# Telling a kernel's own list scheduler how VectorE and GpSimd share an SBUF port, with durations and due times set anew

## The chip, the cores and the metric

One core of one Trainium2 chip. The metric is the device time of one execution in microseconds (us), lower is better. "Before" and "after" are the two kernels; L1023 is line 1023 of the kernel at hand, and lines move by five between before and after.

## The reference, cut to what matters

Four graph layers over 128 graphs of 64 nodes with 256 features, in float32:

```python
h = relu(layernorm(x)); x = x + attention(h, adj)             # layer 0: 8 heads, masked by adj
h = relu(layernorm(x)); x = x + attention(h, log(adj + 1e-6)) # layer 1
h = relu(layernorm(x)); x = x + ggnn(h, adj)                  # layer 2: 5 steps of aggregate and GRU
h = relu(layernorm(x)); x = x + elu(gated_gcn(h, adj))        # layer 3
```

The graphs are handled in 16 groups of four pairs. Three groups are in work at any time: one in its attention layers ("front"), one or two in their GRU steps, one in layer 3 ("back"). Names in the lines below: q, k, v, s, e and aT belong to attention (aT is a transpose of the weights e on TensorE), agg to the aggregation over neighbours, gb, gc, nb, nc and sn to the GRU, l3b, l3c and F to layer 3, lnT, hT and hx are transposes, xn is a normalised input. SBUF and PSUM are the two on-chip memories; in this kernel TensorE's results land in PSUM.

## The kernel before

The kernel records every operation with an engine, an estimated cost, its inputs and outputs and a due time ("key"), and a list scheduler in the kernel then decides in which order the operations are emitted. In the runs below each engine takes its operations in the order in which they were emitted: in swap1, where 11 VectorE operations were each moved by one place, only these and the ones they passed change place in the trace. So all of the argument is about numbers that the scheduler believes:

```python
AFTER = {"PE": 210, "DVE": 125, "ACT": 145, "POOL": 90, "SP": 2500}   # ns until a result is seen
TO_PE = 120
BESIDE = 0.2      # weight for a tiled matmul block next to another
TURNING = 0.05
AHEAD = 1.75      # how far past the most urgent key an operation may be placed, in groups
FRONT_SPAN = 0.9  # ... due times of fronts, backs, GRU steps, first groups, fused weights ...
BACK_LAST = 0.85
STEP_SPAN = 0.4
BACK_END = -0.05
FIRST = -1.0

def dve(n, ptr=0):
    return n * 1.042 + 75 + 60 * ptr

# class Plan, run(): one step of the list scheduler
for eng, ops in ready.items():
    for op in ops:
        if op.key > horizon:
            continue
        at = max(clock[eng], op.ready)
        if op.port:                     # GpSimd, and VectorE with two SBUF inputs or in a 2-port mode
            at = max(at, locked["POOL" if eng == "DVE" else "DVE"])
        # ... buffers ...; among those that can start within 15 ns of the first, the most urgent
op.fn()                                 # emits the instruction
end = at + op.cost
if op.port:
    locked[op.eng] = end + 60
```

Operations from the attention layers, the GRU update and layer 3:

```python
vec(120, ... nc.vector.reciprocal(z.tile, z.tile))                    # L766, 128x8
pool(1000, ... nc.gpsimd.tensor_tensor(e8(), e8(), z..., op=ALU.mult))  # L767, then PE transposes e: "aT"
vec2(dve(TOK), ... scalar_tensor_tensor(a_(), a_(), 0.5, b_(), ...))  # L1023; vec2 = needs the port
sca(... Tanh ...)
pool(1230, ... nc.gpsimd.tensor_tensor(b_(), hh(), a_(), op=ALU.subtract))   # L1027
vec2(dve(TOK, 1), ...)                                                # L1029
vec2(dve(TOK, 0.5), ...)                                              # L1031
vec(dve(384), ... tensor_tensor(F..., part(bk), t..., op=ALU.add))    # L1195: one input in PSUM, no port
```

## Time and profile before

| | before |
|---|---|
| time, median of 4 runs | 2582.32 us (2581.43 to 2583.26) |
| span of the profiled run | 2579.5 us |
| TensorE busy | 2526.5 us |
| one group in the repeating part | 156.64 us |

How to read it: PE is TensorE (PEld its weight loads), DVE is VectorE, ACT ScalarE, POOL GpSimd. A group of lines gives the busy time, the mean duration in ns, and after the second bar the idle time of the engine before those instructions and what ended it. A line of the waits gives the waiting operation, what it waited for, the total, the number of times and the longest. TensorE's waits from 400 to 2200 us, the repeating part, are only these:

```profile
PE aT L773 <- POOL e L767: 6.8, 12, 0.6
PE l3c L1183 <- DVE F L1195: 6.1, 11, 0.6
PE qkvc L669 <- DVE v L690: 2.8, 12, 0.2
PE gc L918 <- DVE sg L990: 2.4, 12, 0.4
PE hT L509 <- DVE h L1031: 0.3, 1, 0.3
```

Four waits come back in every group, at the same places. They add up to 18 us of recorded idle.

### The profile page before, as it was taken

The page shows a single profiled execution, that of the slowest core. Times are in us where ns is not written, and L with a number is a line of the kernel's source. Part 1 is how long each engine was busy: PE and PEld are TensorE (multiplying, and loading weights), DVE is VectorE, ACT ScalarE, POOL GpSimd, SP SyncE. Part 2 cuts the span into 40 slices and gives each one's busy share as a digit, 9 for nine tenths or more (in the row PEclk, how much of TensorE's full clock was granted, in tenths as well). Part 3 has the DMA queues.
Part 4 walks back from the last instruction along what each step waited for, and adds up shares of the span by engine and source line. Part 5 has one row for each costly group of instructions (what it writes and reads, how often), then busy time and mean ns, then how long its engine had stood idle before and what let it go on. Part 6 is the DMA issues. An engine that isn't in the chain of part 4 may idle for free.

```text
span 2579.5 us, 58085 instructions
## 1 busy us (share of the span) xinstructions
PE 2526.5 (98%) x23489; PEld 2144.7 (83%) x23489; DVE 2086.3 (81%) x4647; ACT 1401.4 (54%) x2796; POOL 856.8 (33%) x890
## 2 busy tenths in 40 slices
PE   8999999999999999999999999999999999999997
PEld 6788888888888888888888888888888888888885
DVE  5876787888888888888878878888888888876766
ACT  3555555555555555555555565555555555555543
POOL 4533323324323243323323233243232333323220
PEclk9999999999999999999999999999999999999998
DMA  6331222113131122222212221121211122111110
GB/s 207 117 111 53 70 69 78 65 53 99 48 99 62 64 70 69 78 70 69 67 60 78 70 82 64 54 95 48 99 62 64 66 70 78 65 52 65 48 69 17
DMA packets 78256, 188.47 MB, mean 73 GB/s; under 512 B 14802, under 2 KB 66852, under 8 KB 67108
## 3 DMA queue, kind: packets, MB, share of 16 engines
q1 hardware_dynamic: 77872, 184.71, 21.3%
q8 instruction: 186, 3.05, 0.5%
q14 instruction: 82, 0.67, 0.1%
q10 hardware_dynamic: 116, 0.04, 0.0%
HBM read 166.70 MB, written 18.02 MB: 72 GB/s over the span
## 4 chain that ended last, share of the span: by engine, by line
PE 87%; DVE 9%; ACT 2%; issue 1%; POOL 1%; DMA 0%; ACTq 0%; POOLq 0%; DVEq 0%
PE gb L918 19%; PE gc L918 15%; PE nb L918 10%; PE nc L918 7%; PE qkvb L669 5%; PE y L805 4%; PE qkvc L669 4%; PE agg L958 3%; PE s L731 3%; PE l3b L1183 2%; PE hT L509 2%; PE l3c L1183 2%; PE lnT L509 2%; PE o L792 2%; PE aT L773 2%
## 5 line engine op out<-in xcount | busy, mean ns | idle before, releaser
L1027 POOL TENSOR_TENSOR sn<-h,sn 128x512 f32<-128x512 f32 x160 | 212.4, 1328 | 592.7 <-ACT sn L1025 580.9
L918 PE MATMUL gb<-Th,w_hh 128*128 128x256 f32 x960 | 250.6, 383 | 0.3 <-DVE sg L990 0.3
L918 PE MATMUL gb<-Ta,gv 128*128 128x256 f32 x960 | 246.9, 380 | 0.0
L767 POOL TENSOR_TENSOR e<-e,ssum 128x512 f32<-128x512 f32 x128 | 142.2, 1122 | 278.8 <-DVE ssum L766 240.8
L495 POOL TENSOR_TENSOR rstd<-pw,few 128x2 f32<-128x2 f32 x128 | 104.7, 819 | 357.3 <-DVE pw L494 351.4
L887 POOL TENSOR_TENSOR Th<-h 128x256 f32<-128x256 f32 x160 | 116.3, 747 | 311.9 <-PE nb L918 174.7
L918 PEld LDWEIGHTS gb<-Th,w_hh 128*128 128x128 f32 x960 | 174.3, 190 | 26.2 <-issue 0.8
L918 PEld LDWEIGHTS gb<-Ta,gv 128*128 128x128 f32 x960 | 176.1, 190 | 21.3
L918 PE MATMUL gc<-h,w_hh 128*128 128x256 f32 x640 | 167.4, 384 | 0.1
L918 PE MATMUL gc<-agg,gv 128*128 128x256 f32 x640 | 164.4, 379 | 0.0
L535 DVE TENSOR_SCALAR xn<-x,mv,rstd 128x256 f32<-128x256 f32 x256 | 125.4, 525 | 31.1 <-POOL rstd L495 15.6
L1029 DVE SCALAR_TENSOR_TENSOR sn<-sg,sn 128x512 f32<-128x512 f32 x160 | 109.5, 684 | 50.6 <-POOL sn L1027 50.5
L1010 ACT ACTIVATE sg<-sg,b_rz 128x512 f32<-128x512 f32 x160 | 109.3, 716 | 74.3 <-DVE sg L990 74.3
L1025 ACT ACTIVATE sn<-sn,b_n 128x512 f32<-128x512 f32 x160 | 115.4, 722 | 56.6 <-DVE sn L1023 55.9
L1021 DVE SCALAR_TENSOR_TENSOR sn<-sg,sn 128x512 f32<-128x512 f32 x160 | 135.8, 849 | 12.3 <-ACT sn L1075 7.8
L918 PE MATMUL nb<-Th,w_hh 128*128 128x256 f32 x480 | 144.6, 383 | 0.0
L918 PE MATMUL nb<-Ta,gv 128*128 128x256 f32 x480 | 143.1, 380 | 0.0
L887 POOL TENSOR_TENSOR Th<-h,Th 128x256 f32<-128x256 f32 x160 | 138.1, 863 | 11.5 <-DVE h L1031 5.8
L805 PE MATMUL y<-w_L_gnn_Wo,oT 128*128 128x256 f32 x512 | 135.1, 383 | 0.5 <-DVE oT L800 0.5
L918 PEld LDWEIGHTS gc<-agg,gv 128*128 128x128 f32 x640 | 119.3, 190 | 17.9 <-issue 0.2
L1031 DVE SCALAR_TENSOR_TENSOR h<-sn 128x512 f32<-128x512 f32 x160 | 128.4, 802 | 2.8
L1023 DVE SCALAR_TENSOR_TENSOR sn<-sn 128x512 f32<-128x512 f32 x160 | 128.4, 802 | 0.9
(207 smaller groups left out, 6832.7 us busy)
## 6 DMA issues: line engine op xcount, KB each, us to landing
gv<-gates SPq DMA_DIRECT2D x80, 1344.0 KB, 5.8
qw<-kept SPq DMA_DIRECT2D x203, 192.0 KB, 2.4
x<-in_x_dram SPq DMA_DIRECT2D x32, 256.0 KB, 3.0
out_dram<-x SPq DMA_DIRECT2D x32, 256.0 KB, 2.5
gates<-gv SPq DMA_DIRECT2D x5, 1344.0 KB, 5.2
adjq<-in_adj_dram SPq DMA_DIRECT2D x8, 256.0 KB, 3.0
gw<-in_L_gnn_weight_dram SPq DMA_DIRECT2D x5, 256.0 KB, 5.9
kept<-s SPq DMA_DIRECT2D x8, 128.0 KB, 1.8
```

What stands on the lines that cost most here:

```text
L535: vec2(325, lambda p=p, i=i: nc.vector.tensor_scalar(xn[:, i, :], xt[:, p, :], mv[:, i, 0:1], rstd[:, i : i + 1], op0=ALU.subtract, op1=AL ...
L669: nc.tensor.matmul(bk[:, j * P : (j + 1) * P], lhs, rhs, start=first and j == 0, stop=True, skip_group_check=True)
L767: pool(1000, lambda e8=e8, z=z: nc.gpsimd.tensor_tensor(e8(), e8(), z[:, :, None].to_broadcast(shape), op=ALU.mult), [e, z], [e])
L805: pe(mm(256), lambda i=i, c=c: nc.tensor.matmul(py[:, i * D : (i + 1) * D], oT[:, i, c, :], w_o[:, c, :], start=c == 0, stop=c == 1), [(oT ...
L887: pool(690, lambda: nc.gpsimd.tensor_tensor(T[:, i, :], x(), y(), op=ALU.subtract), reads, [(T, i)])
L918: nc.tensor.matmul(bank_[:, col * HALF : (col + 1) * HALF], at(g, n), rhs(), start=first and j == 0, stop=True, skip_group_check=True)
L1021: vec2(dve(TOK), lambda: nc.vector.scalar_tensor_tensor(a_(), r(), 1.0, a_(), op0=ALU.add, op1=ALU.mult), [*ts[0], n_v], [n_v])
L1023: vec2(dve(TOK), lambda: nc.vector.scalar_tensor_tensor(a_(), a_(), 0.5, b_(), op0=ALU.mult, op1=ALU.add), [n_v], [n_v])
L1025: sca(act(TOK, 1.5), lambda: nc.scalar.activation(a_(), a_(), AF.Tanh, bias=b_n[:, oc : oc + 1]), [n_v, b_n], [n_v])
L1027: pool(1230, lambda: nc.gpsimd.tensor_tensor(b_(), hh(), a_(), op=ALU.subtract), [*hp, n_v], [n_v])
L1029: vec2(dve(TOK, 1), lambda: nc.vector.scalar_tensor_tensor(b_(), z(), 1.0, b_(), op0=ALU.add, op1=ALU.mult), [*ts[1], n_v], [n_v])
L1031: vec2(dve(TOK, 0.5), lambda: nc.vector.scalar_tensor_tensor(hh(), b_(), 0.5, a_(), op0=ALU.mult, op1=ALU.add), [n_v], hp)
```

## The change

Its intent: a scheduler that expects port conflicts where they happen. GpSimd now counts as asking for the port when its data is there (it is picked first and delayed then), holds end a little before the operations do, the tiny power operations hold the port only at their start, costs are brought nearer to the recorded ones, and the weights, the run-ahead and all due times are set anew. No operation is added or removed.

```diff
-TO_PE = 120
+TO_PE, TO_POOL = 120, 60
+HOLD = {"DVE": 60, "POOL": 95}
-BESIDE = 0.2
+BESIDE = 0.5
-TURNING = 0.05
-AHEAD = 1.75
+TURNING = 0.15
+AHEAD = 2.15
-FRONT_SPAN = 0.9
+FRONT_SPAN = 0.95
-BACK_LAST = 0.85
-BACK_SPAN = 0.6
+BACK_LAST = 0.45
+BACK_SPAN = 0.65
-STEP_SPAN = 0.4
+STEP_SPAN = 0.5
-BACK_END = -0.05
-ENTRY = 0.05
-FIRST = -1.0
-FIRST_SPAN = 1.1
+BACK_END = 0.1
+ENTRY = 0.25
+FIRST = -1.2
+FIRST_SPAN = 1.15
-FUSE_SPAN = 0.45
+FUSE_SPAN = 0.4
-    return n * 1.042 + 75 + 60 * ptr          # dve
+    return n * 1.042 + 68 + 60 * ptr
-    return n * 0.833 + 70 + 90 * ptr          # act
+    return n * 0.833 + 60 + 105 * ptr
-        return op.lat
+        return op.lat + (TO_POOL if user.eng == "POOL" and op.eng == "DVE" else 0)
-                    if op.port:
-                        at = max(at, locked["POOL" if eng == "DVE" else "DVE"])
+                    if op.port and eng == "DVE":
+                        at = max(at, locked["POOL"])
             op.fn()
+            if op.port and op.eng == "POOL":
+                at = max(at, locked["DVE"])
-                locked[op.eng] = end + 60
+                locked[op.eng] = end - HOLD[op.eng] if op.port == 1 else at
-        pool(680 if n == 2 else 1220, ... op=ALU.pow
+        pool(660 if n == 2 else 970, ... op=ALU.pow ... port=2)
-        pool(1560, ... bias addition
+        pool(1225, ... bias addition
-                vec2(dve(TOK, 1), ...
+                vec2(dve(TOK), ...
 ... (further costs: bn_stats, bn_aggr, reciprocal, one activation, a copy, the vec2 of L1031)
```

More of the change, by code (lines that the diff above doesn't have):

```diff
@@ L309, in sca, with pool @@
         plan.add("ACT", cost, fn, reads, writes, early=early)
-    def pool(cost, fn, reads, writes, early=0.0):
-        plan.add("POOL", cost, fn, reads, writes, early=early, port=True)
+    def pool(cost, fn, reads, writes, early=0.0, port=1):
+        plan.add("POOL", cost, fn, reads, writes, early=early, port=port)
     def dma(kb, fn, reads, writes, n=1):
@@ L494, in power @@
         vec2(70, lambda: nc.vector.tensor_scalar(s.tile, at(), eps, None, op0=ALU.add), [src], [s])
-        pool(680 if n == 2 else 1220, lambda: nc.gpsimd.tensor_tensor(dst.tile, s.tile, few[:, 1 : 1 + n], op=ALU.pow),
-             [s, (few, 1)], [dst])
+        pool(660 if n == 2 else 970, lambda: nc.gpsimd.tensor_tensor(dst.tile, s.tile, few[:, 1 : 1 + n], op=ALU.pow),
+             [s, (few, 1)], [dst], port=2)
     def transposed(dst, dst_at, src, src_at, name, on_act, writes, relu=False, early=0.0,
@@ L528, in norm_relu_t @@
             p = 2 * half + i
-            vec(345, lambda p=p, i=i: nc.vector.bn_stats(st[:, i, :], xt[:, p, :]), [(xt, p)], [(st, i)])
-            vec(95, lambda i=i: nc.vector.bn_aggr(mv[:, i, :], st[:, i, :]), [(st, i)], [(mv, i)])
+            vec(332, lambda p=p, i=i: nc.vector.bn_stats(st[:, i, :], xt[:, p, :]), [(xt, p)], [(st, i)])
+            vec(83, lambda i=i: nc.vector.bn_aggr(mv[:, i, :], st[:, i, :]), [(st, i)], [(mv, i)])
         power(rstd, mv, lambda: mv[:, :, 1], EPS, 2, name)
@@ L743, in attend @@
             pe(860, scores, [qk, k_exp], pss, holds=es, mode=T64)
-        pool(1560, lambda: nc.gpsimd.tensor_tensor(
+        pool(1225, lambda: nc.gpsimd.tensor_tensor(
             xt[:, pp : pp + 2, :], xt[:, pp : pp + 2, :], bo[:, None, :].to_broadcast([P, 2, D]),
@@ L765, in attend @@
                 [e], [z])
-            vec(120, lambda z=z: nc.vector.reciprocal(z.tile, z.tile), [z], [z])
+            vec(109, lambda z=z: nc.vector.reciprocal(z.tile, z.tile), [z], [z])
             pool(1000, lambda e8=e8, z=z: nc.gpsimd.tensor_tensor(
@@ L1016, in update @@
                             last, lambda k=k: last[:, k * HALF : (k + 1) * HALF])
-                        sca(act(HALF, 1), lambda k=k, col=col, half=half, at=at: nc.scalar.activation(
+                        sca(act(HALF, 1.4), lambda k=k, col=col, half=half, at=at: nc.scalar.activation(
                             g_v[:, half, k, :], at(), AF.Tanh, bias=b_rz[:, col : col + 1], scale=0.5),
@@ L1028, in update @@
                      [*hp, n_v], [n_v])
-                vec2(dve(TOK, 1), lambda: nc.vector.scalar_tensor_tensor(
+                vec2(dve(TOK), lambda: nc.vector.scalar_tensor_tensor(
                     b_(), z(), 1.0, b_(), op0=ALU.add, op1=ALU.mult), [*ts[1], n_v], [n_v])
-                vec2(dve(TOK, 0.5), lambda: nc.vector.scalar_tensor_tensor(
+                vec2(dve(TOK), lambda: nc.vector.scalar_tensor_tensor(
                     hh(), b_(), 0.5, a_(), op0=ALU.mult, op1=ALU.add), [n_v], hp)
@@ L1108, in front @@
             s = slice(gp * NODES, (gp + 1) * NODES)
-            pool(530, lambda s=s: nc.gpsimd.tensor_copy(blk[s, :, s], adjq[s, sel, :]), [adjq], [(blk, gp)])
+            pool(350, lambda s=s: nc.gpsimd.tensor_copy(blk[s, :, s], adjq[s, sel, :]), [adjq], [(blk, gp)])
         A = new("A", [P, PAIRS, NODES], 3, f"A_{g}")
```

## The prediction

> **What bounds the kernel now.** I read the page's engine table, then the chain of work that ended last, then TensorE's waits and its timeline over one repeating stretch, then the groups of VectorE and GpSimd.
>
> ```profile
> PE 2526.5 (98%) x23489; PEld 2144.7 (83%) x23489; DVE 2086.3 (81%) x4647; ACT 1401.4 (54%) x2796; POOL 856.8 (33%) x890
> ...
> PE 87%; DVE 9%; ACT 2%; issue 1%; POOL 1%; DMA 0%; ACTq 0%; POOLq 0%; DVEq 0%
> ```
>
> TensorE (PE) is busy 98% of 2579.5 us and makes up 87% of the chain. A gain must therefore come out of TensorE's gaps, or from cheaper matmuls. Its busy figure hides part of the gaps, because a matmul's recorded span reaches over the start of the next one; so I price matmuls by the distance between starts. The timeline of TensorE in the repeating part (start, time, engine, line, operation, tile, count, idle before) shows both a price and a gap:
>
> ```profile
> 1245.09 1.03 PE L918 MATMUL gb<-Ta,gv 128*128 128x256 f32 x4
> 1245.95 0.59 PE L918 MATMUL nb<-Th,w_hh 128*128 128x256 f32 x2
> 1246.38 0.60 PE L773 MATMUL aT<-ident,e 128*128 128x128 f32 x4
> 1247.22 0.71 PE L669 MATMUL qkvc<-hTQ,qw 128*128 128x128 f32 x4 [0.24 <-DVE v L690]
> 1247.77 0.39 PE L669 MATMUL qkvc<-qw,hTQ 128*128 128x128 f32 x2
> 1248.72 0.66 PE L773 MATMUL aT<-ident,e 128*128 128x128 f32 x4 [0.56 <-POOL e L767]
> ```
>
> Four 256-column matmuls take 0.86 us from start to start, 0.216 each. The four transposes at 1246.38 should take 4 x 0.109 = 0.44 and the next work starts 0.84 later: a 0.40 us gap, of which the record calls 0.24 idle. Priced like this over the whole trace (medians: 0.216, 0.111, 0.322 and 0.429 us for 256, 128, 384 and 512 columns, 0.109 for a transpose; tiled blocks by their means, 0.015, 0.027 and 0.011 us for agg, s and o, plus about 0.1 to enter a tiled block and 0.14 to 0.19 to leave it), TensorE's work is: 1,632 us of 256-column matmuls, 266 of 128, 135 of 384, 24 of 512, 191 of transposes, 175 of tiled ones, 48 of mode changes: **2472 us**. Outside it lie 8.3 us before the first matmul, about 8 after the last, and some **92 us of gaps**. By part of the run, counting only gaps over 40 ns: 19 in the first 400 us, 46 from 400 to 2200, 3 to 2500, 18 in the tail.
>
> From 400 to 2200 us the chain repeats: 128x256 blocks of gc stand at 836.49, 993.10, 1149.78 and 1306.39 us, so one group of four graph pairs takes 156.6 us. Its priced work is 152.3, so **4.3 us per group are gaps**. TensorE's waits between 993.10 and 1149.78 us, which is one such group:
>
> ```profile
> PE aT L773 <- POOL e L767: 0.6, 1, 0.6
> PE l3c L1183 <- DVE F L1195: 0.6, 1, 0.6
> PE gc L918 <- DVE sg L990: 0.3, 2, 0.2
> PE qkvc L669 <- DVE v L690: 0.2, 1, 0.2
> ```
>
> By starts, these four are 0.73, 0.73, 0.33 and 0.40 us; an hT transpose adds 0.26, and eleven gaps of 0.10, each with a wait just before it, nearly all the rest.
>
> **What the Trainium skill says.** (1) SBUF — State Buffer, section Who interferes with whom: VectorE and GpSimd share one port pair; it is an exclusive lock, and a VectorE instruction with two SBUF inputs or in a 2-port mode and a GpSimd instruction that reads SBUF block each other in the order of issue. The trace agrees. Groups of 128x512 VectorE operations with equal shapes:
>
> ```profile
> L1029 DVE SCALAR_TENSOR_TENSOR sn<-sg,sn 128x512 f32<-128x512 f32 x160 | 109.5, 684 | 50.6 <-POOL sn L1027 50.5
> L1021 DVE SCALAR_TENSOR_TENSOR sn<-sg,sn 128x512 f32<-128x512 f32 x160 | 135.8, 849 | 12.3 <-ACT sn L1075 7.8
> L1031 DVE SCALAR_TENSOR_TENSOR h<-sn 128x512 f32<-128x512 f32 x160 | 128.4, 802 | 2.8
> ```
>
> L1029 waits for GpSimd's result, so it rarely meets a GpSimd operation: 684 ns. L1021 and L1031 meet them: means 849 and 802, with medians of 689 and 684 and maxima above 1600. The same happens to GpSimd: the multiplication at L767 has a median of 1043 ns, and took 1.51 us just before the 0.56 us wait above. That wait is port contention reaching TensorE. (2) Perfetto Trace Analysis, section Tensor Engine Instruction: TensorE's end times are estimated from the instruction's size, not observed. The trace agrees (four matmuls "1.03 us" long start 0.86 us apart), which is why starts are used. (3) The same page, section GPSIMD Engine Instruction, advises against trusting a GpSimd span. Here medians and minima differ by 1% (1272 and 1262 ns at L1027), so I use them, but with care.
>
> **The change, part by part.** No instruction is added or removed. Each engine has as many instructions in the built program as before (12,621 on TensorE, 4649 VectorE, 2804 ScalarE, 895 GpSimd); only their order moves, on every engine. The order is made by a list scheduler in the kernel, and the change makes its inputs truer.
>
> - Costs: the GpSimd subtraction stays 1230 ns (median 1272), the bias addition goes from 1560 to 1225 (1322 measured), the small powers from 680/1220 to 660/970 (706/1017), a block copy from 530 to 350 (398). VectorE's fixed part drops from 75 to 68.
> - Port: before, the scheduler held GpSimd back until VectorE had let the port go when choosing what to place, and added 60 ns to every hold. Now GpSimd asks when its data is there, the hold ends 60 or 95 ns before the operation does, and the tiny powers hold it only at their start (they take 706 ns for two columns). This should stop the scheduler's surprises, such as the 1.51 us multiplication.
> - Weights for staying in a tiled mode, due times, a longer run-ahead (1.75 to 2.15 groups).
>
> *Cost of TensorE's work.* I counted mode changes in both built orders. Entries into tiled blocks from plain work: 169 before, 175 after; switches between the two tile sizes 38 and 31. At the prices above, 48.3 against 48.6 us. So the stronger preference for tiled neighbours buys nothing: **+0.3 us**, and one group's work becomes 152.4 us.
>
> *The gaps of the repeating part.* The new order repeats exactly from group to group; the old one alternates slightly. What I can count is how much TensorE work lies between a producer and its consumer. For l3c's second product after the first, whose wait cost 0.73 us, it is 1.3 us before and 1.5 after, and to the third 0.9 before and 3.0 after. From agg to the first gb product on Ta the smallest distance is 5.1 before and 9.4 after; from the hT transpose to agg 1.8 and 3.1. In layer 0's second half the distance from s to aT falls from 9.3 to 7.3, but VectorE has less queued there (10 operations, 6.1 us of medians, instead of 14 and 7.5). Against that, qkvc still has a turnaround of 1.7 us in one half (as the one that cost 0.40), and one aT now stands 16.1 us behind s with 16.5 us of VectorE medians between (before, such sums came out some 15% above the measured time: 8.3 for 7.0 us). I judge that half of the 4.3 us goes: 2.1 us a group left. Over 13 groups that repeat or nearly do: 13 x 2.1 = **-27 us**.
>
> *Head and tail.* The first agg block comes after 103.3 us of priced work instead of 104.8: about -1. In the tail the last GRU product of the last group ends 19.6 us of work before the end instead of 21.1, and from it to the end runs a chain of 42 us that filler does not shorten: **+1.5**. One transpose that waited 1.31 us moves behind other work: **-1**. Sum: 2581.7 + 0.3 - 27 - 1 + 1.5 - 1, so about **2555**; I put 2557, as re-tuning to a model seldom gains all it promises.
>
> **Rivals.** (a) *The gaps only move.* VectorE is busy 85% of a group (132.5 of 156.7 us), its own waits are short, and a scheduler that packs it against 1.7 us turnarounds may create as many misses as it mends. For it: the old scheduler also believed its plan. Against it: the sizes put in are nearer the records. It would make 2575 to 2590. (b) *All gaps go.* For it: they are few, the same in each group, and each under 0.75 us. Against it: 37 us of head and tail come from data dependencies. At most 13 x 4 = 52 us, so 2530. (c) *A longer run-ahead starves something:* buffers or the queue of weight loads make TensorE wait for DMA. Against it: only 8.3 us of TensorE's waits are for DMA, all before the first matmul, and DMA is 21% busy. It would cost 10 to 30 us.
>
> **Range and chances.** The gap left per group decides: 0.8 us gives about 2538, 3.8 about 2577. So 2538 to 2577, eight times in ten. Faster by 2% needs under 2530, which is rival (b) in full and more: 0.03. Slower by 2% means 51 us more gaps: 0.01.
>
> **What would show it right or wrong.** Right: equal instruction counts, a group period of 154 to 155.5 us, TensorE's busy time nearly unchanged with gaps at aT and l3c gone, VectorE's L1021, L1023 and L1031 (moved by five lines) with lower means. Wrong: a period of 156 or more with waits under new names (rival a), waits for DMA (c), or a head or tail that changes by over 8 us.

## The result, and the profile after

The changed kernel takes **2537.85 us** (median of 4 runs, 2536.72 to 2538.85) against 2582.32: 44.5 us less. Ratios here are the mean time of one kernel's runs over that of the other's of the same rounds, so not quite the ratio of the medians: 0.9828, 95% interval 0.9811 to 0.9845. The predicted time was 2557, and the measured one lies just outside the low end of the range.

The head of the page of after:

```profile
PE 2507.0 (99%) x23489; PEld 2142.7 (85%) x23489; DVE 2047.8 (81%) x4647; ACT 1396.5 (55%) x2796; POOL 865.1 (34%) x890
...
PE 95%; DVE 3%; ACT 1%; DMA 0%; issue 0%; POOL 0%; SPq 0%; DVEq 0%; ACTq 0%; POOLq 0%
```

As many instructions, and the chain is now 95% TensorE instead of 87%. The busy times of the engines from 400 to 2200 us (PE, PEld, DVE, ACT, POOL, granted clock, DMA share, GB/s), first before, then after:

```profile
400.00:2200.00 1800.00, 1780.63 (x16914) 1522.94 (x16913) 1521.54 (x3348) 1004.17 (x2022) 601.90 (x609) 1.00 0.21 70
```

```profile
400.00:2200.00 1800.00, 1800.00 (x17224) 1552.16 (x17223) 1488.01 (x3415) 1016.36 (x2066) 613.97 (x617) 1.00 0.22 72
```

After, TensorE is busy for all of the 1800 us, does 310 more matmuls in them, and its list of waits there is empty. VectorE does 67 more operations in 33.5 us less.

By starts of the first agg block of each group, the 44.6 us between the two profiled spans divide like this (us):

| part of the run | before | after | difference |
|---|---|---|---|
| start to the third group | 360.6 | 355.5 | -5.1 |
| third to thirteenth group (ten groups) | 1565.0 | 1537.1 | -27.9 |
| thirteenth to sixteenth | 427.8 | 424.6 | -3.2 |
| sixteenth to the last matmul | 218.4 | 210.3 | -8.1 |
| last matmul to the end | 7.7 | 7.4 | -0.3 |

Waits are not all that changed in the head and the tail. The profile also records the granted clock, the share of its full clock that TensorE was given (third figure from the end in these lines). Two of the four stretches of before, ahead of its last matmul, in which it was about half; then, in after, the same stretch of the head, and the tail up to its last matmuls:

```profile
45.10:51.90 6.80, 5.93 (x76) 4.48 (x77) 2.12 (x4) 0.99 (x2) 6.57 (x7) 0.50 0.65 204
2547.00:2550.40 3.40, 3.40 (x7) 1.71 (x6) 1.61 (x3) 0.98 (x2) 0.00 (x0) 0.51 0.18 62
```

```profile
45.10:51.90 6.80, 6.45 (x54) 4.66 (x55) 4.96 (x13) 1.68 (x4) 6.80 (x7) 1.00 0.68 186
2500.50:2530.70 30.20, 21.62 (x78) 12.33 (x76) 27.20 (x82) 13.27 (x29) 2.91 (x3) 1.00 0.08 27
```

The other two stretches of before are 2512.9 to 2516.3 and 2557.3 to 2560.7 us. Matmuls in them take twice their price: the pair of 384 columns at 2548.17 us starts 1.28 us before the next pair, 0.64 for each, against 0.322. By these prices the half clock costs before about 3.2 us in the head, 1.7 between the sixteenth group and the last GRU product, and 3.1 behind that product; after, nothing. So by this estimate some 8 of the 44.6 us are clock and not waits. In all profiled runs such stretches stand only before 160 us or after 2480 us; those of before come behind waits of TensorE of 2.1, 1.4, 4.6 and 1.8 us, and its repeating part, whose longest wait is 0.6 us, has none. That the waits bring the clock down was not tested.

One group takes 153.93 us instead of 156.64, with 152.43 priced as before. The VectorE groups that the prediction pointed to, after:

```profile
L1026 DVE SCALAR_TENSOR_TENSOR sn<-sg,sn 128x512 f32<-128x512 f32 x160 | 119.9, 757 | 38.5 <-ACT sn L1080 35.7
L1028 DVE SCALAR_TENSOR_TENSOR sn<-sn 128x512 f32<-128x512 f32 x160 | 114.2, 720 | 1.5
L1036 DVE SCALAR_TENSOR_TENSOR h<-sn 128x512 f32<-128x512 f32 x160 | 109.7, 692 | 2.6
L976 DVE TENSOR_TENSOR Ta<-agg,Ta 128x256 f32<-128x256 f32 x160 | 97.8, 611 | 1.5
```

The three operations of the GRU update fall to 757, 720 and 692 ns (849, 802 and 802 before). But the subtractions that make Ta rise from 456 to 611 ns. Counting every VectorE operation that took over 100 ns more than the 15th percentile of its kind, 288 were lengthened before, by 189 us in all, and 308 after, by 139 us; on GpSimd 187 by 67 us and 250 by 73 (a kind is one line, one set of tiles, one shape). Every one of them overlaps an operation of the other engine. **There are not fewer port conflicts, though together they cost 44 us less of the two engines' time. From 400 to 2200 us TensorE waits for none of them.**

### The profile page after: what moved, and what is told of

It reads as the page before. It is cut to its first block, busy times and chain, and to the rows that moved or that the text cites.

```text
span 2534.9 us, 58088 instructions
## 1 busy us (share of the span) xinstructions
PE 2507.0 (99%) x23489; PEld 2142.7 (85%) x23489; DVE 2047.8 (81%) x4647; ACT 1396.5 (55%) x2796; POOL 865.1 (34%) x890
## 4 chain that ended last, share of the span: by engine, by line
PE 95%; DVE 3%; ACT 1%; DMA 0%; issue 0%; POOL 0%; SPq 0%; DVEq 0%; ACTq 0%; POOLq 0%
PE gb L923 22%; PE gc L923 16%; PE nb L923 11%; PE nc L923 8%; PE qkvb L674 6%; PE qkvc L674 5%; PE y L810 4%; PE agg L963 3%; PE l3b L1188 3%; PE s L736 3%; PE l3c L1188 2%; PE hT L514 2%; PE lnT L514 2%; PE aT L778 2%; PE o L797 2%; PE hom L1251 1%
## 5 line engine op out<-in xcount | busy, mean ns | idle before, releaser
L1032 POOL TENSOR_TENSOR sn<-h,sn 128x512 f32<-128x512 f32 x160 | 207.3, 1299 | 549.2 <-ACT sn L1030 549.2
L892 POOL TENSOR_TENSOR Th<-h 128x256 f32<-128x256 f32 x160 | 126.6, 811 | 243.8 <-PE nb L923 166.5
L1026 DVE SCALAR_TENSOR_TENSOR sn<-sg,sn 128x512 f32<-128x512 f32 x160 | 119.9, 757 | 38.5 <-ACT sn L1080 35.7
L1034 DVE SCALAR_TENSOR_TENSOR sn<-sg,sn 128x512 f32<-128x512 f32 x160 | 109.5, 690 | 40.0 <-POOL sn L1032 39.6
L976 DVE TENSOR_TENSOR Ta<-agg 128x256 f32<-128x256 f32 x160 | 90.0, 578 | 55.5 <-PE nb L923 43.5
L923 PEld LDWEIGHTS gc<-h,w_hh 128*128 128x128 f32 x640 | 117.8, 190 | 16.4 <-ACT sg L1022 0.5
L987 ACT ACTIVATE p5g<-gc 128x512 f32<-128x512 f32 x80 | 47.7, 596 | 145.7 <-PE gc L923 102.3
```

The lines of the kernel that those rows point to most:

```text
L892: pool(690, lambda: nc.gpsimd.tensor_tensor(T[:, i, :], x(), y(), op=ALU.subtract), reads, [(T, i)])
L923: nc.tensor.matmul(bank_[:, col * HALF : (col + 1) * HALF], at(g, n), rhs(), start=first and j == 0, stop=True, skip_group_check=True)
L1026: vec2(dve(TOK), lambda: nc.vector.scalar_tensor_tensor(a_(), r(), 1.0, a_(), op0=ALU.add, op1=ALU.mult), [*ts[0], n_v], [n_v])
L1032: pool(1230, lambda: nc.gpsimd.tensor_tensor(b_(), hh(), a_(), op=ALU.subtract), [*hp, n_v], [n_v])
L1034: vec2(dve(TOK), lambda: nc.vector.scalar_tensor_tensor(b_(), z(), 1.0, b_(), op0=ALU.add, op1=ALU.mult), [*ts[1], n_v], [n_v])
```

## The experiments

Two theories at the start. A: the truer model of the port and the durations removed the gaps, whatever the due times. B: the new due times and run-ahead made the gain, and the model is only along. A third, C: each order is a draw, and the result is the best of many. Gains below are given as ratios to the kernel before, run on the same chip in the same rounds (its medians: 2582.43, 2581.45, 2581.65 and 2581.54 us in the four sets); the changed kernel stands at 0.9828. Every output was correct.

### Which part of the change: the model or the due times

Only the model (port rule and costs), with the old weights, run-ahead and due times:

```diff
 # before, with
+TO_POOL, HOLD, the new port rule, port=2, all new costs
```

> New port rule and new durations, with the weights, due times and run-ahead of before. Theory A (a truer model of the port and the durations removes the gaps, whatever the due times): group period near 154 us in the mean of two groups (the order alternates), gaps of TensorE over 40 ns in the repeating part 1 to 2 us a group, time 2540 to 2550. Theory B (the newly set due times and run-ahead made the gain, the model is only along): period 156 to 157, time 2575 to 2585. Theory C (each order is a draw; the result is the best of many): anything, also slower than before.

Measured: 2587.04 us, ratio 1.0018 (1.0002 to 1.0035). No gain at all. By parts: a group takes 155.61 us in the mean (156.64 before), and the ten groups from the third to the thirteenth take 1551.2 us, 13.8 less; but the third group's agg comes at 383.5 us instead of 360.6. TensorE's longest wait in the first 360 us, apart from the first load, is this:

```profile
PE aT L778 <- POOL e L772: 11.6, 3, 6.5
```

Three transposes wait 11.6 us for GpSimd's multiplication in the first groups (2.9 before). That is 8.7 of the 22.9 us; other waits make some 6.5, and 6 are clock: 27.3 us of this head run at half clock, 6.8 before. Theory A falls as stated.

Only the weights, run-ahead and due times, with the old model:

```diff
 # before, with
+BESIDE, TURNING, AHEAD and all due times of after
```

> Weights, due times and run-ahead of after, with the old port rule and old durations. Theory A: period 156 to 157 us, four gaps of 0.3 to 0.7 us a group left at aT, l3c, gc or qkvc, time 2570 to 2582; only head and tail shorter. Theory B: period near 154, time 2538 to 2548. Theory C: anything.

Measured: 2566.49 us, ratio 0.9939 (0.9924 to 0.9954); a group takes 155.57 us. Neither theory: 16 us of the 44.5.

Without the port rule, and without the costs:

```diff
 # after, with
-HOLD, TO_POOL, the new port rule and port=2      (port_old)
 # after, with
-all new costs                                    (durations_old)
```

> The changed kernel with the old port rule and old holds alone put back. If the port rule is what counts: most of the gaps return, period 155.5 to 157, time 2562 to 2580. If the durations count instead: period about 154, time within 8 us of the changed kernel (2530 to 2546).

> The changed kernel with the old durations alone put back. If the durations are what counts: period 155.5 to 157, time 2562 to 2580. If the port rule counts: period about 154, time 2530 to 2546. If both are needed: both this and the run with the old port rule lie about half-way, 2550 to 2565.

Measured: port_old 2568.25 us, ratio 0.9946, 154.99 us a group; durations_old 2552.33 us, ratio 0.9885, 154.66 us a group. With the new due times, the costs alone bring nothing (2566.5 to 2568.3), the port rule alone 14 us (2566.5 to 2552.3), and the costs on top of the port rule another 14 us (2552.3 to 2537.9). So the parts act together. The trace qualifies this for the repeating part: there the costs alone do bring 0.6 us a group (155.57 to 154.99), lost again in the head and behind the thirteenth group.

The runs so far suggest a fourth theory, D: model and due times gain only together. Whether the due times of the repeating part belong to this:

```diff
 # after, with
-FRONT_SPAN = 0.95, BACK_SPAN = 0.65, STEP_SPAN = 0.5, ENTRY = 0.25
+FRONT_SPAN = 0.9, BACK_SPAN = 0.6, STEP_SPAN = 0.4, ENTRY = 0.05
```

> The changed kernel with the due times of the repeating part put back (front, back and step spans, entry). Theory A (model and due times act each by itself): period 154 to 154.5, time 2538 to 2548. Theory D (the truer model needs due times set to it, the two act together): period 155 to 156.6, time 2552 to 2580.

Measured: 2559.34 us, ratio 0.9914 (0.9899 to 0.9928), 155.61 us a group, the same as model_new_dues_old. Both figures lie where theory D (the two parts need each other) put them, but D holds only in part: in the repeating part the new model alone gives 1.0 us a group, the new due times alone 1.1, both 2.7, so most of that gain adds up and 0.6 us a group needs both. What needs both above all is the head, which the new model alone lengthens by 23 us.

### Head and tail

```diff
 # after, with
-FIRST = -1.2, FIRST_SPAN = 1.15, FUSE_SPAN = 0.4
+FIRST = -1.0, FIRST_SPAN = 1.1, FUSE_SPAN = 0.45      (head_old)
 # before, with the new model and
+FIRST = -1.2, FIRST_SPAN = 1.15, FUSE_SPAN = 0.4      (model_new_head_new)
```

> The changed kernel with the due times of the first groups and of the weight fusing put back (-1.0, 1.1, 0.45). Only rows 12 to 1290 of TensorE differ. If these made the 5 us of the head: third group's agg at 360 us or later instead of 355.5, time 2543 or more; since the new model with all old due times reached it at 383.5, up to +28 is possible (2565). If the head owes its gain to the model: within 2 us of 2538.

> New port rule and durations with the old weights, run-ahead and due times, but the new due times of the first groups and of the weight fusing. The same kernel without these lost 23 us before the third group. If that loss comes from due times that do not fit the truer model: agg of the third group at 355 to 362 us instead of 383.5, time 2558 to 2566. If it comes from the run-ahead or the weights: 380 us or later, time about 2585.

Measured: head_old 2551.84 us, ratio 0.9884; the third group's agg at 369.8 us instead of 355.5, and all later parts as in after within 0.1 us. model_new_head_new 2564.12 us, ratio 0.9933; 359.1 us instead of the 383.5 of the same kernel with the old head. So the 23 us that the new model lost there were due times that did not fit it, and three numbers gave them back. In head_old's 14.3 us, 8 are recorded waits and 5.8 are matmuls in 13.7 us at half clock.

```diff
 # after, with
-BACK_LAST = 0.45, BACK_END = 0.1
+BACK_LAST = 0.85, BACK_END = -0.05
```

> The changed kernel with the two due times of the last backs put back (0.85 and -0.05). In the built order only the last 68 of 12,621 rows of TensorE and the last 96 of VectorE differ. If these two due times shortened the tail: last GRU product to the end 41 us again instead of 34.4, time +6 to +8, so 2544 to 2546. If the tail got shorter by the truer costs or by what stands before it: within 2 us of 2538.

Measured: 2549.79 us, ratio 0.9877 (0.9862 to 0.9892). The time from the last GRU product to the end, 41.7 us before and 34.4 after, is 47.0 here, worse than in either, and 12 us instead of the 6 to 8 expected. TensorE's waits from 2440 us on, first in after, then in tail_old:

```profile
PE l3b L1188 <- ACT hT L519: 2.2, 2, 1.5
PE lnT L514 <- DVE xn L540: 2.0, 2, 1.1
```

```profile
PE hx L1224 <- DVE h L1036: 6.5, 1, 6.5
PE lnT L514 <- DVE xn L540: 4.0, 2, 3.1
```

With the old due times the last group's transposes back to tokens (hx) wait 6.5 us for the last GRU result and those of the last layer norm 4.0. From 2506.5 to 2520.2 us, from within the wait of 6.5 on, the granted clock was 0.50, which makes some 4.5 of the 12 us. In the kernel before, the longest waits of the tail (from 2500 us on) were others:

```profile
PE l3b L1183 <- DVE hTT L1172: 4.6, 1, 4.6
PE lnT L509 <- DVE xn L535: 4.5, 3, 1.8
```

So 12 us hang on two due times. model_old_dues_new, with the old model, reached 35.2 us from the last GRU product to the end: the tail's gain is the due times', with the old model as with the new.

### Are the two largest gaps of before port conflicts at all?

To test the mechanism without another draw of the scheduler, I recorded the exact order of before and moved single VectorE operations in it; the instructions of all other engines stand as before (the traces of swap1, swap2 and swap3 have TensorE, ScalarE and GpSimd in the order of before). The stretch around the aT gap, in before (VectorE and GpSimd lines of the timeline):

```profile
1246.49 0.41 DVE L688 TENSOR_TENSOR qk<-qkvc,q 128x256 f32<-128x256 f32 x1
1246.83 0.18 DVE L766 RECIPROCAL ssum<-ssum 128x8 f32<-128x8 f32 x1
1246.93 0.23 DVE L690 TENSOR_TENSOR v<-qkvc,q 128x128 f32<-128x128 f32 x1
...
1247.09 0.68 DVE L1023 SCALAR_TENSOR_TENSOR sn<-sn 128x512 f32<-128x512 f32 x1
1247.15 1.51 POOL L767 TENSOR_TENSOR e<-e,ssum 128x512 f32<-128x512 f32 x1 [1.33 <-DVE ssum L766]
...
1247.69 1.13 DVE L653 TENSOR_TENSOR hTQ<-hT,hTQ 128x128 f32<-128x128 f32 x1
```

L1023 starts 0.06 us before GpSimd's multiplication, which then takes 1.51 us (median of its kind 1.043), and the next VectorE operation on the port takes 1.13 us for 0.28 of work, until GpSimd is done. The move: the reciprocal ahead of the addition L688, which reads PSUM and needs no port.

```diff
 # order of before, in 11 groups
+  L766 reciprocal (ssum of the last head block)
   L688 qk addition
-  L766 reciprocal
   L690 v addition
   L1023
```

> The kernel before with its exact order on every engine, but in 11 groups VectorE's 8-column reciprocal (L766) stands one place earlier, ahead of a 256-column addition from PSUM. GpSimd then asks for the port before VectorE's next operation with two SBUF inputs. If the 0.73 us wait of the aT transpose is port contention: the multiplication of GpSimd there takes 1.04 us instead of 1.51, the wait and the short gap after it go, period 155.8 instead of 156.64, time -8 to -9 (2572 to 2574). If the gap only moves to another wait: period within 0.2 of 156.6, time within 2 us of before.

Measured: 2574.8 us, ratio 0.9973 (0.9959 to 0.9988), 155.99 us a group. The same stretch in swap1:

```profile
1244.02 0.20 DVE L793 RECIPROCAL ssum<-ssum 128x8 f32<-128x8 f32 x1
1244.14 0.37 DVE L715 TENSOR_TENSOR qk<-qkvc,q 128x256 f32<-128x256 f32 x1
1244.36 1.04 POOL L794 TENSOR_TENSOR e<-e,ssum 128x512 f32<-128x512 f32 x1 [1.12 <-DVE ssum L793]
1244.43 0.28 DVE L717 TENSOR_TENSOR v<-qkvc,q 128x128 f32<-128x128 f32 x1
1244.62 1.33 DVE L1050 SCALAR_TENSOR_TENSOR sn<-sn 128x512 f32<-128x512 f32 x1
```

Now GpSimd has the port first and takes 1.04; L1023 (here L1050) waits and takes 1.33, and nothing on TensorE waits for it. The 0.73 us gap is gone; the qkvc wait just before it grew from 0.40 to 0.53. The time gained, 6.9 us and 0.65 a group, is a little under the forecast. The lock is in it, but the move did two things: from the start of the pair L688 and L766, GpSimd begins after 0.34 us instead of 0.66, as its input is ready sooner, and takes 1.04 us instead of 1.51. So 0.47 of the 0.79 us by which the multiplication ends sooner are port contention, and 0.32 are the reciprocal's place in the queue.

The l3c gap. In before, an xn operation meets a GpSimd subtraction, and the addition F that TensorE waits for stands five places behind it:

```profile
1284.70 1.46 DVE L535 TENSOR_SCALAR xn<-x,mv,rstd 128x256 f32<-128x256 f32 x1
1284.74 1.26 POOL L1027 TENSOR_TENSOR sn<-h,sn 128x512 f32<-128x512 f32 x1 [2.07 <-ACT sn L1025]
...
1287.41 0.54 DVE L1195 TENSOR_TENSOR F<-l3c,l 128x384 f32<-128x384 f32 x1
```

```diff
 # order of before, in 11 groups
-  L535 xn
   L1172 hTT   (port)
   L653 hTQ    (port)
   L990 sg     (one input in PSUM)
   L688 qk     (one input in PSUM)
   L1195 F     (one input in PSUM)
+  L535 xn
```

> The kernel before with its exact order, but in 11 groups one xn operation of VectorE, which took 1.47 us because it met a GpSimd subtraction of 1.27 us, stands five places later, after the addition of l3c that it held up. If the 0.73 us wait of l3c is port contention: that wait and its 0.10 us follower go, period 155.8, time -8 to -9. If the gap moves: within 2 us of before.

> Both moves at once. If the two gaps are independent and both are contention: period 155.0, time -16 to -18 (2564 to 2566). If mending one makes the other worse: less than -10.

Measured: swap2 2579.76 us, ratio 0.9992 (0.9977 to 1.0007), a miss; the gap shrank only from 0.73 to 0.52 us, because the subtraction hTT now met GpSimd and took 1.34 us. swap12 2572.83 us, ratio 0.9966: swap1's gain and little more. Up to here the reading is open: contention, or only a long queue. So the next move fills the blocked time with operations that need no port:

```diff
 # order of before, in 10 groups
-  L535 xn, L1172 hTT, L653 hTQ
   L990 sg
   L688 qk
+  L1172 hTT, L653 hTQ
   L1195 F
+  L535 xn
```

> The kernel before with its exact order, but in 10 groups three VectorE operations that need the shared port (xn and two subtractions) stand behind the two that read one operand from PSUM and need no port; those two run while GpSimd's subtraction of 1.27 us holds it. Moving xn alone (swap2) only put the next such operation in its place (1.34 us) and cut the gap from 0.73 to 0.52. If l3c's gap is port contention: the gap and its 0.10 us follower go, period 155.8, time -6 to -9. If it is only the length of VectorE's queue: gap 0.4 or more, time within 3 us of before.

> This move together with that of swap1, which took 0.65 us a group. If the two gaps are independent: period 155.1 to 155.3, time -14 to -16 (2566 to 2568).

Measured: swap3 2573.6 us, ratio 0.9969 (0.9958 to 0.9980), 155.82 us a group, and the l3c gap is gone. swap13 2566.86 us, ratio 0.9945 (0.9930 to 0.9960), 155.16 us a group: 14.7 us, about the sum of the two (6.9 and 7.9). Of TensorE's waits from 400 to 2200 us, those of aT and l3c are left only once each in swap13, in place of 12 and 11 times:

```profile
PE aT L813 <- POOL e L807: 0.6, 1, 0.6
PE l3c L1223 <- DVE F L1235: 0.5, 1, 0.5
```

The stretch in swap3:

```profile
1282.56 0.69 DVE L1028 TENSOR_TENSOR sg<-gb,p5g 128x512 f32<-128x512 f32 x1
1282.60 1.27 POOL L1065 TENSOR_TENSOR sn<-h,sn 128x512 f32<-128x512 f32 x1 [2.07 <-ACT sn L1063]
1283.16 0.42 DVE L726 TENSOR_TENSOR qk<-qkvc,q 128x256 f32<-128x256 f32 x1
1283.49 0.53 DVE L1210 TENSOR_TENSOR hTT<-hT,hTT 128x128 f32<-128x128 f32 x1
```

VectorE's two operations with one input in PSUM take 0.69 and 0.42 us while GpSimd has the port (their medians before are 0.69 and 0.41), and F starts 1.58 us after the first of them (1284.14 against 1282.56), where in before it started 2.71 us after xn. In swap2 and swap3 the same five operations stand ahead of F, with xn behind it; only their order differs. So the 0.52 us by which swap3 beats swap2 are contention and not a shorter queue. The gaps at gc, qkvc and hT, most of the other 1.2 of the 2.7 us a group, were not tested by such moves.

### Weights and run-ahead

```diff
 # after, with
-BESIDE = 0.5, TURNING = 0.15
+BESIDE = 0.2, TURNING = 0.05                          (weights_old)
-AHEAD = 2.15
+AHEAD = 1.75                                          (ahead_old)
+AHEAD = 2.6                                           (ahead_long)
```

> The changed kernel with the two weights for tiled neighbours put back (0.2 and 0.05). 334 of 12,621 TensorE rows differ, none in the repeating groups. By the count of mode changes these weights are worth nothing: within 2 us of 2538. If they matter: 3 us or more slower.

> The changed kernel with the run-ahead put back to 1.75. Rows 26 to 10,698 of 12,621 of TensorE differ, mostly by a few places. If the longer run-ahead lets the scheduler fill gaps: 3 to 12 us slower, 2541 to 2550. If it only adds freedom that is not used: within 2 us of 2538.

> The changed kernel with a still longer run-ahead, 2.6 instead of 2.15, as a version that might beat both. The step from 1.75 to 2.15 was worth 4.7 us, 3.5 of it in the head. If more helps further: 2533 to 2537. If it is used up, or lets late work crowd out what is due: 2537 to 2550.

Measured: weights_old 2536.89 us, ratio 0.9829: nothing, as the count of mode changes said. ahead_old 2542.58 us, ratio 0.9849, and ahead_long 2543.29 us, ratio 0.9854: about 5 us slower on either side, 3.5 and 4.7 of them before the third group (about 1.7 and 3.0 of that is half clock), at 153.90 to 154.00 us a group. So 2.15 is set to the rest of the numbers; no version here beats the changed kernel clearly. As to theory C, orders did differ by some us in the head and tail for small edits; but the two gaps were mended one by one by moves chosen from the trace, so the repeating part's gain is not luck alone.

## Why the prediction was wrong

- **What bounds the kernel, and where a gain must come from:** right. TensorE's priced work is 2472 us in both orders, and the gain is gaps, except that some 8 us of what the prediction counted as gaps in the head and tail were matmuls at half the granted clock.
- **Cost of mode changes, +0.3 us, and the weights worth nothing:** right (weights_old).
- **The gaps as port contention:** right for the two largest, shown by swap1 for about 0.5 us of the one and by swap3 against swap2 for 0.5 us of the other, of 0.73 each. The sentence that eleven gaps of 0.10 us each had "a wait just before it" is wrong. After *every* exit from a tiled block, in both kernels, the second matmul starts 0.104 us late, or 0.056 us if the first ones are transposes: 169 exits with 15.7 us before, 175 with 15.8 after. That is a price of leaving a tiled block that I had counted among the gaps. Of the 4.3 us a group only some 3.3 could go, and 2.7 went.
- **The step "half of the 4.3 us goes: 2.1 us a group left", -27 us over 13 groups:** mechanism right, size a little low, and the half a judgement: 1.5 us left, of which about 1.0 is the price of leaving tiled blocks, and -31.1 us from the third to the sixteenth group. About 4 us of the miss.
- **The step "Head ... about -1":** wrong, -5.1. I counted TensorE's work before the first agg and not the waits in the first groups, which head_old and model_new_head_new show to react by 14 to 24 us to three due times. About 3.2 us of it are the half clock that is gone, 2.7 are recorded waits (other spacings give back 0.7). Another 4 us of the miss.
- **The step "a chain of 42 us that filler does not shorten", +1.5, and -1 for a moved transpose:** wrong, -8.1. The 42 us were not a fixed chain of dependencies. They held waits made by the order, 4.6 us of them for one subtraction queued on VectorE, and, behind these waits, 6.8 us at half clock, which the prediction had priced at full clock; they became 34.4. Of the 7.3 us, 2.5 are recorded waits, 3.1 clock and 1.4 less TensorE work. tail_old shows 12 us hanging on two due times. This is the largest term of the miss, 8.6 us, and one of the signs of being wrong that the prediction named (a head or tail that changes by over 8 us).
- **The 2 us taken off as "re-tuning to a model seldom gains all it promises":** a guess without a number, in the wrong direction.
- **Rivals:** (a), gaps that only move, did happen in parts of the change (model_new_dues_old, swap2), not in the whole. (b) came nearest for the repeating part. (c) did not happen: DMA waits stayed at 8.3 us, before the first matmul.
- **VectorE's lower means:** seen, but not because there were fewer conflicts; the lengthened operations became more, and other ones.

What stays open: why the new costs bring nothing with the old port rule and 14 us with the new one was not followed down to single gaps, and the three due times of the head were only tested as a block. What brings the granted clock down in head and tail was not tested. Theory C was not tested by drawing other orders from the same numbers.

## What to carry to other kernels

If engines share a lock, ask who waits for the one that loses, and fill the blocked time with operations that don't need the lock; moving one operation away often puts the next in its place. A scheduler's model and its due times must be set together: here the truer model alone gained nothing in all, as the head lost what the repeating part won, and the head and tail, under a quarter of the run, held 13 of 44 us, 8 of them by the clock. Price the gaps first by what can't be removed (mode exits), and treat a "dependency chain" at the end as fixed only after checking each wait in it.

## What the Trainium skill lacked or had wrong

- SBUF — State Buffer, section Who interferes with whom: what it says of the lock held in the cases looked at (a GpSimd multiplication of 1.04 us taking 1.51 beside a VectorE operation with two SBUF inputs, a VectorE xn of 0.41 us taking 1.46 beside GpSimd), and so did its statement that a VectorE operation with at most one SBUF input stays clear of GpSimd (swap3: 0.69 and 0.42 us, not lengthened). Who issued first could not be read from recorded starts: the xn that lost starts 0.04 us before GpSimd's subtraction. The section does not say what follows for an order: removing one loser puts the next one on the lock (swap2: 1.34 us for a subtraction of 0.28).
- TensorE: Matmul & The Clock Gate, section Part 3: Packing small matmuls — row/col tiling: it gives the gain of tiled blocks and the cost of semaphores, but no price for switching, and no other page has one. Here entering a tiled block cost about 0.09 us, leaving it 0.14 to 0.19, and the second matmul after leaving another 0.104 (0.056 among transposes), 175 times in a run.
- Perfetto Trace Analysis, section GPSIMD Engine Instruction: nothing here contradicts its warning about GpSimd spans, but for these elementwise operations the spans were usable: the median of L1027 is 1272 ns and the minimum 1262, and the transpose that waited for the multiplication of 1.51 us starts 0.06 us after its recorded end (1248.72 against 1248.66).
